# Attention probabilities brought to their keys' partitions by VectorE transposes and a copy through DRAM, in place of transposes by DMA

## The chip, the cores and the metric

The kernel runs on one core of a Trainium2 chip. A core has TensorE (PE: matmuls, with weight loads, PEld, beside them), VectorE (DVE), ScalarE (ACT), GpSimd (POOL) and SyncE (SP), which here only issues DMAs; 16 DMA engines move the data. Each engine works through its own instructions in order and waits on semaphores. The metric is the time of one execution on the device, in microseconds (us).

## The reference

One transformer layer on x of 2048 x 512 (f32): multi-head latent attention, a residual and a layer norm, then one linear layer with bias, a residual and a layer norm.

```python
cq = rms_norm(x @ w_qa.T)                                   # 2048 x 384
q_nope, q_pe = split((cq @ w_qb.T).reshape(s, 16, 192))     # 128 + 64 a head, rotary on q_pe
ckv_l, k_pe = rms_norm(...), rope(...)                      # of x @ w_kva.T: 128 + 64
k_nope, v = split((ckv_l @ w_kvb.T).reshape(s, 16, 256))
scores = (q_full @ k_full.T) * 192 ** -0.5                  # 16 heads, causal
out = softmax(scores) @ v @ w_o.T
x = layernorm(x + out)
x = layernorm(x + x @ (weight * scale_weight[:, None]).T + bias)
```

## The kernel before, in words

The keys' and values' up-projections are folded into the queries and the output, so scores are taken against the shared latent (`Kn`, 128 rows) and the rotary part (`Kp`), and the values are the latent itself (`V`). Every f32 operand of a matmul is split into a high and a low part; a score is five matmuls (`score`, L409 to L427, the matmuls on L421). The causal mask is added on the diagonal 128 columns either by a bf16 matmul in the middle of the five (L423: block 0, and block 3's first head of a pair) or by a VectorE addition in the score bank (L427).

Queries come in four **blocks** b of 512, heads in eight **pairs** p, and a block in four **query tiles** qt of 128. A tile needs nk = (4b + qt + 1) x 128 keys: 128 to 512 in block 0 and 1664 to 2048 in block 3. One (b, p, qt) is called a **unit** here. `units` (L626) runs over p, then qt, then the two heads j.

For a head in blocks 1 to 3, `head_scores` (L432) makes the scores, takes the negated maximum (L459, VectorE), the bias (L466 or L468), the exponentials into `pr` with their sums (L474, ScalarE), and the reciprocal of the sum (`inv`, L484 to L487). `head_probs` (L490) scales `pr` into f16 high words (L495, ScalarE) and the f16 remainder (L498, VectorE); both stand in one tile `hl`, first all high words, then all low words. Then one `dma_start_transpose` a head on SP (L502) moves `hl`, queries on partitions, into `PT`, keys on partitions. `head_probs` is a generator that is advanced while the next head's scores are made, so these steps interleave with the next head's maximum. In block 0, `pair_scores` and `pair_probs` (L507, L529) do the same for both heads at once, with the transpose on L535.

`values` (L540) multiplies V with both heads' words: for each 128 keys three matmuls of 256 columns (L551), in two halves, then a copy to `ot` (L556) and a store (`put_off`). A unit's product is put off: `run_values(lag)` runs half of an older unit's product after each head's scores, with a lag of 3, 3 and 2 units in blocks 1, 2 and 3. TensorE's queue therefore holds, in block 3: scores of unit u's first head, first half of the product of unit u-2, scores of the second head, second half, and so on. `PT` is a part of `ring`, 12 x 2048 half-words a partition, which holds three units in block 3.

The order is written by hand for TensorE and SP from block 1 on, and for VectorE and ScalarE too from block 3's second tile on; elsewhere the scheduler of the language orders VectorE and ScalarE. SP's queue holds, in order, the transposes, the `ot` stores and the loads of projected weights (`wq`, `wpe`).

After the last block an output stage runs from L770: it accumulates 512 columns for each 128 tokens over 8 pairs (`accumulate`), adds the residual, normalises (`layer_norm`, L847), transposes, applies the linear layer (`ffn`, L867) and normalises again. `rsqrt` (L193) is an addition and a power on GpSimd. In `ffn`, GpSimd adds bias and residual beforehand (`xb`, L874).

Of the kernel before, what the change touches and what calls it, by code (L numbers as in the profile page):

```python
# [9 lines left out]
F16 = mybir.dt.float16  # L10
BF16 = mybir.dt.bfloat16
F32 = mybir.dt.float32
F32R = mybir.dt.float32r
AF = mybir.ActivationFunctionType
ALU = mybir.AluOpType
# [34 lines left out]
def mla_block(ctx: ExitStack, tc: tile.TileContext, a, out):  # L50
# [45 lines left out]
    ctx_kv = ctx.enter_context(ExitStack())  # L96
    kv = ctx_kv.enter_context(tc.tile_pool(name="kv", bufs=1))
# [12 lines left out]

    blk = ctx.enter_context(tc.tile_pool(name="blk", bufs=2, side="right"))
# [72 lines left out]
    def value_output(p, pool, tag):  # L184

        wvo = state["wvo"][p]
        for j in range(2):
# [3 lines left out]
            yield  # L191

# [216 lines left out]
    def score(ps, c0, w, b, p, j, qt, masked):  # L409
# [7 lines left out]
        by_product = b == 0 or b == 3 and j == 0  # L417
        ops = [(qh, Kn, 0), (qh, Kn, 1), (ql, Kn, 0), (qp, Kp, 0), (qp, Kp, 1)]
        n = 0
        for lhs, K, i in ops:  # L420
            nc.tensor.matmul(ps[:, :w], lhs, K[:, i, c0 : c0 + w], start=n == 0, stop=n == 4)  # L421
            if n == 1 and masked is not None and by_product:
                nc.tensor.matmul(ps[:, masked : masked + P], identb, maskb, start=False, stop=False)  # L423
            n += 1
        if masked is not None and not by_product:
            dg = ps[:, masked : masked + P]
            nc.vector.tensor_tensor(dg, dg, maskb, ALU.add)  # L427
# [4 lines left out]
    def head_scores(pools, b, p, j, qt, nk, prev):  # L432
# [38 lines left out]
        pr = pools[1].tile([P, nk], F32, tag="pr", name=f"pr{b}_{p}_{qt}_{j}", bufs=4 if b == 1 else 2)  # L471
# [17 lines left out]

    def head_probs(pools, b, p, j, qt, nk, PT, pr, inv):  # L490
        hl = pools[0].tile([P, 2, nk], F16, tag="hl", name=f"hl{b}_{p}_{qt}_{j}", bufs=(6, 4, 2)[b - 1])
# [5 lines left out]
        for c in cuts:  # L497
# [3 lines left out]
        n2 = 2 * nk  # L501
        nc.sync.dma_start_transpose(  # L502
            PT[:, j * n2 : (j + 1) * n2].rearrange("p (k q) -> p k q", q=P), hl.rearrange("p a c -> p (a c)")
        )
        put_in()

    def pair_scores(pool, b, p, qt, nk):  # L507
# [4 lines left out]
        for j in range(2):  # L512
            score(ps[:, j, :], 0, w, b, p, j, qt, nk - P)
# [15 lines left out]
    def pair_probs(pool, b, p, qt, nk, PT, pr, inv):  # L529
        hl = pool.tile([P, 2, 2, nk], F16, tag=f"hl{qt}", name=f"hl{b}_{p}_{qt}")  # L530
        for j in range(2):
# [3 lines left out]
        nc.sync.dma_start_transpose(  # L535
            PT[:, : 4 * nk].rearrange("p (k q) -> p k q", q=P), hl.rearrange("p j a c -> p (j a c)")
        )
        yield

    def values(b, p, qt, nk, PT):  # L540

        kts = nk // P
        v = PT[:, : 4 * nk].rearrange("p (j a k q) -> p j a k q", j=2, a=2, k=kts)
# [297 lines left out]
    def load_fw(kt):  # L841
        raw = pc.tile([P, HID], F32, tag="xb", name=f"fraw{kt}", bufs=2)
        nc.scalar.dma_start(raw, a["fw"][:, kt])
        nc.vector.tensor_tensor(raw, raw, fsc, ALU.mult)
# [142 lines left out]
```

## Time and profile before

| | us |
|---|---|
| median of 3 runs | 1588.22 (1586.73 to 1588.98) |
| the profiled execution | 1588.17 |
| its span, first to last instruction | 1586.4 |

| part of the span | from | to | length |
|---|---|---|---|
| block 0, with the first projections | 0 | 253.6 | 253.6 |
| block 1 | 253.6 | 495.5 | 241.9 |
| block 2 | 495.5 | 851.9 | 356.4 |
| block 3 | 851.9 | 1328.7 | 476.8 |
| output stage | 1328.7 | 1586.4 | 257.7 |

A row of the groups reads: line, engine, operation, written tile <- read tiles, shapes (partitions x elements a partition), count | busy us in all, mean ns of one | idle time of the engine just before them, and what ended it. Matmuls overlap, so a mean duration (273 ns for a product with V) is longer than the distance from one start to the next (109 ns, taken from the starts in the trace). "SPq" rows are DMA issues; the transposes held SP's queue 3353 ns each in the median for `ring`. Of the 633,032 DMA packets 557,056 have 256 B: the transposes'. The granted TensorE clock was 0.993 in the mean.

### The profile page before, as it was taken

The numbers are of one execution on the slowest core, as the hardware profiler recorded it, in microseconds if no ns is written. First come the engines' busy times: TensorE is split into PE (matmuls) and PEld (weight loads), VectorE is DVE, ScalarE is ACT, GpSimd is POOL, SyncE is SP. The second block draws the span as 40 slices with busy tenths as digits, with TensorE's granted clock in tenths as the row PEclk, the third lists the DMA queues.
The fourth block names the chain that finished last, engine by engine and source line by source line (L and its number), as shares of the span: only waits on it lengthen the run. The fifth ranks groups of instructions, "written<-read, shape, count | busy, mean of one in ns | idle before, by whom it ended". The sixth has DMA issues, their size and how long they took to land. (4 is left out here: it accounts for less than half of the span.)

```text
span 1586.4 us, 24671 instructions
## 1 busy us (share of the span) xinstructions
PE 1546.3 (97%) x9130; PEld 1291.1 (81%) x9130; DVE 1161.2 (73%) x2099; ACT 924.7 (58%) x1631; POOL 361.5 (23%) x434
## 2 busy tenths in 40 slices
PE   8899998999999999999999999999999999999997
PEld 7688877888887788888888788888888886788886
DVE  6777777878787978787786877877777775465564
ACT  5767776665665676666765665665666665311120
POOL 2243325154016204050032401400400000022132
PEclk9999999999999999999999999999999999999999
DMA  7879877788897987788897888878678798433230
GB/s 230 258 197 240 191 191 160 147 176 190 149 218 163 173 163 165 159 162 170 160 204 148 168 145 168 156 143 165 140 143 176 148 233 196 146 118 122 94 113 33
DMA packets 633032, 262.49 MB, mean 165 GB/s; under 512 B 570288, under 2 KB 611376, under 8 KB 631888
## 3 DMA queue, kind: packets, MB, share of 16 engines
q1 hardware_dynamic: 621472, 233.62, 68.8%
q0 software_dynamic: 4672, 17.73, 3.6%
q10 hardware_dynamic: 6768, 9.57, 2.1%
q8 instruction: 72, 1.18, 0.3%
q14 instruction: 48, 0.39, 0.1%
HBM read 83.17 MB, written 35.13 MB: 75 GB/s over the span
## 5 line engine op out<-in xcount | busy, mean ns | idle before, releaser
L421 PE MATMUL s<-Kn,qn 128*128 128x512 f32 (+4 forms) x1920 | 521.1, 376 | 9.4 <-ACT pr L474 4.4
L474 ACT ACTIVATE pr<-s,bias,rq 128x1024 f32<-128x1024 f32 (+3 forms) x320 | 324.4, 1017 | 217.0 <-DVE bias L468 157.2
L498 DVE SCALAR_TENSOR_TENSOR hl<-pr,inv,hl 128x1024 f16<-128x1024 f32 (+7 forms) x320 | 359.6, 1137 | 38.7 <-ACT hl L495 34.9
L421 PEld LDWEIGHTS s<-Kn,qn 128*128 128x128 f32 x1920 | 339.5, 190 | 55.7 <-ACT pr L474 7.4
L551 PEld LDWEIGHTS <-V 128*128 128x128 f16 x3264 | 302.5, 98 | 86.6 <-issue 47.6
L551 PE MATMUL o<-ring,V 128*128 128x256 f16 x3024 | 362.9, 273 | 2.5 <-DVE qn L68 1.2
L421 PE MATMUL s<-Kp,pe 128*128 128x512 f32 (+4 forms) x1280 | 361.4, 363 | 0.0
L495 ACT ACTIVATE hl<-pr,inv 128x1024 f16<-128x1024 f32 (+7 forms) x320 | 294.6, 961 | 91.3 <-issue 34.5
L459 DVE TENSOR_REDUCE neg<-s 128x1 f32<-128x1024 f32 (+3 forms) x320 | 317.8, 993 | 38.0 <-PE s L421 34.9
L421 PEld LDWEIGHTS s<-Kp,pe 128*128 128x128 f32 x1280 | 234.0, 189 | 29.6
L359 POOL TENSOR_TENSOR prod<-prod 128x512 f32<-128x512 f32 x15 | 19.4, 1292 | 639.1 <-DVE prod L352 639.0
L391 PE MATMUL ps_qn<-cq,wq 128*128 128x512 f32 x576 | 145.1, 397 | 3.1 <-ACT ot L556 1.7
L770 PE MATMUL acc<-wvo,oh 128*128 128x512 f32 x448 | 143.9, 402 | 1.8 <-ACT pr L474 1.8
L374 POOL TENSOR_TENSOR pe<-prod,ph 32x512 fp32r<-32x512 f32 x92 | 138.8, 1509 | 6.0
L391 PEld LDWEIGHTS ps_qn<-cq,wq 128*128 128x128 f32 x576 | 107.3, 190 | 24.8 <-ACT ot L556 2.4
L770 PEld LDWEIGHTS acc<-wvo,oh 128*128 128x128 f32 x448 | 83.1, 188 | 23.2 <-issue 3.8
L486 DVE TENSOR_SCALAR inv<-sums 128x1 f32<-128x1 f32 x128 | 27.0, 211 | 97.5 <-ACT pr L474 97.5
L770 PE MATMUL acc<-wvo,ol 128*128 128x512 f32 x224 | 88.1, 393 | 0.0
L556 ACT ACTIVATE ot<-o 128x256 f32<-128x256 f32 x128 | 48.4, 378 | 45.2 <-PE o L551 39.6
L347 PE MATMUL ps_pe<-cq,wpe 128*128 128x512 f32 x288 | 73.8, 402 | 0.2 <-DMA cq<-cq_d 0.2
L64 ACT ACTIVATE oh<-o 128x1024 fp32r<-128x1024 f32 x28 | 29.7, 1060 | 65.6 <-PE acc L770 50.0
L65 DVE TENSOR_TENSOR ol<-o,oh 128x1024 fp32r<-128x1024 f32 x28 | 38.8, 1387 | 39.3 <-ACT oh L64 39.3
(147 smaller groups left out, 1631.6 us busy)
## 6 DMA issues: line engine op xcount, KB each, us to landing
wq<-wq_d SPq DMA_DIRECT2D x22, 768.0 KB, 5.7
o<-ot_d SPq DMA_DIRECT2D x32, 512.0 KB, 3.3
ot_d<-ot SPq DMA_DIRECT2D x97, 128.0 KB, 2.4
wpe<-wpe_d SPq DMA_DIRECT2D x10, 768.0 KB, 5.4
wq<-wq_d POOLq DMA_DIRECT2D x9, 768.0 KB, 6.4
cq_d<-cqst SPq DMA_DIRECT2D x18, 256.0 KB, 4.8
wo<-in_wo_dram SPq DMA_DIRECT2D x4, 1024.0 KB, 5.3
x<-in_x_dram SPq DMA_DIRECT2D x16, 256.0 KB, 3.7
```

The source lines that it names most:

```text
L65: nc.vector.tensor_tensor(l, ps, h.bitcast(F32), ALU.subtract)
L347: nc.tensor.matmul(ps, w[:, i, lt, x * P : (x + 1) * P], cq[:, k, lt, :], start=n == 0, stop=n == 8)
L374: (nc.gpsimd if not quick or (b, g) == (0, 0) and j % 2 else nc.vector).tensor_tensor(pe[64 + 32 * x : 96 + 32 * x, j, :], rp[q, x, :], ph ...
L391: nc.tensor.matmul(ps, w[:, i, lt, j * P : (j + 1) * P], cq[:, k, lt, :], start=n == 0, stop=n == 8)
L421: nc.tensor.matmul(ps[:, :w], lhs, K[:, i, c0 : c0 + w], start=n == 0, stop=n == 4)
L459: nc.vector.tensor_reduce(neg[:, ti : ti + 1], v, axis=AX.XY, op=ALU.max, negate=True)
L474: nc.scalar.activation(pr[:, c0 : c0 + n * w].rearrange("p (a c) -> p a c", a=n), v, AF.Exp, bias=bias, scale=r, accum_out=sums[:, ti : ti ...
L495: nc.scalar.activation(hl[:, 0, c], pr[:, c], AF.Copy, scale=inv)
L498: nc.vector.scalar_tensor_tensor(hl[:, 1, c], pr[:, c], inv, hl[:, 0, c], ALU.mult, ALU.subtract)
L551: nc.tensor.matmul(ps[:, :256], vt[:, i, k % 4, :], v[:, :, l, k, :], start=n == 0, stop=n == 3 * kts - 1)
L556: nc.scalar.activation(ot, ps[:, :256], AF.Copy)
L770: nc.tensor.matmul(acc, l[:, t, c], state["wvo"][p][:, i, j, :], start=p == 0 and j == 0 and n == 0, stop=p == NPAIR - 1 and j == 1 and n ...
```

## The change

The two halves of a probability, f16 high and f16 low, now lie side by side in one 32-bit word, so that a move of words moves both. VectorE transposes such words within squares of 32 x 32 (`turn`, into the `pr` tile, which is free by then), a DMA writes the squares to a DRAM tile `sq`, and, when both heads of a pair are written, four DMAs read it back, each filling 32 partitions of `PT` (`gather`). In `values` the moving operand then takes every second half-word.

```diff
+    def turn(words, sq, dst):
+        nc.vector.transpose(
+            sq.rearrange("p (k c r) -> p c k r", k=4, r=32), words.rearrange("p (c k r) -> p c k r", k=4, r=32)
+        )
+        nc.sync.dma_start(dst, sq.rearrange("p (k x) -> p k x", k=4))
+
+    def gather(PT, src):
+        for k in range(4):
+            nc.sync.dma_start(
+                PT[32 * k : 32 * k + 32].bitcast(F32).rearrange("p (q x) -> p q x", q=4),
+                src[:, k].rearrange("(q p) x -> p q x", q=4),
+            )
+
     def head_probs(pools, b, p, j, qt, nk, PT, pr, inv):
-        hl = pools[0].tile([P, 2, nk], F16, tag="hl", name=f"hl{b}_{p}_{qt}_{j}", bufs=(6, 4, 2)[b - 1])
+        words = pools[0].tile([P, nk], F32, tag="hl", name=f"hl{b}_{p}_{qt}_{j}", bufs=(4, 3, 2)[b - 1])
+        hl = words.bitcast(F16).rearrange("p (n a) -> p a n", a=2)
...
-        n2 = 2 * nk
-        nc.sync.dma_start_transpose(
-            PT[:, j * n2 : (j + 1) * n2].rearrange("p (k q) -> p k q", q=P), hl.rearrange("p a c -> p (a c)")
-        )
+        if j == 0:
+            state["sq"] = dram.tile([P, 4, nk // 2], F32, tag=f"sq{b}", name=f"sq{b}_{p}_{qt}", bufs=4)
+        sq = state["sq"]
+        turn(words, pr, sq[:, :, j * nk // 4 : (j + 1) * nk // 4])
+        if j == 1:
+            gather(PT, sq)
         put_in()
...
     def values(b, p, qt, nk, PT):
-        v = PT[:, : 4 * nk].rearrange("p (j a k q) -> p j a k q", j=2, a=2, k=kts)
+        v = PT[:, : 4 * nk].rearrange("p (q j k r a) -> p j a k q r", j=2, q=4, a=2, k=kts)
```

`pair_probs` changes likewise, with one transpose and one write for both heads. The number of `pr` tiles goes from 4, 2, 2 to 5, 3, 2 in blocks 1, 2 and 3, that of `hl` from 6, 4, 2 to 4, 3, 2. Two tiles of 32 B a partition (`pad_l`, `pad_r`) move all later tiles to multiples of 64 B.

The mask by matmul moves behind the five matmuls of a score; in block 0 both heads' scores come first, then both masks.

```diff
-            nc.tensor.matmul(ps[:, :w], lhs, K[:, i, c0 : c0 + w], start=n == 0, stop=n == 4)
-            if n == 1 and masked is not None and by_product:
-                nc.tensor.matmul(ps[:, masked : masked + P], identb, maskb, start=False, stop=False)
+            nc.tensor.matmul(ps[:, :w], lhs, K[:, i, c0 : c0 + w], start=n == 0, stop=n == 4 and not by_product)
+
+        def mask():
+            nc.tensor.matmul(ps[:, masked : masked + P], identb, maskb, start=False, stop=True)
```

In the output stage the value products are made for two pairs at a time (`value_outputs`, from pair 2 on), the residual of the linear layer is put into its weights (the identity is added to their diagonal squares), the bias is added with the matmul's result, and the addition in `rsqrt` of a layer norm goes to VectorE. The last tile gets its bias by two matmuls with one row, is normalised in two halves, and stored by SP and ScalarE.

```diff
+        dg = raw[:, kt * P : (kt + 1) * P]
+        nc.vector.tensor_tensor(dg, dg, ident, ALU.add)
...
-        rsqrt(r, mv[:, 1:2], 1, 1e-5)
-        nc.vector.tensor_scalar(dst, src, mv[:, 0:1], r, ALU.subtract, ALU.mult)
+        t = small.tile([P, 1], F32, tag="lnt", name="lnt")
+        nc.vector.tensor_scalar(t, mv[:, 1:2], 1e-5, None, ALU.add)
+        nc.gpsimd.tensor_tensor(r, t, nhalf[:, :1], ALU.pow)
+        for i in range(parts):
+            c = slice(i * HID // parts, (i + 1) * HID // parts)
+            nc.vector.tensor_scalar(dst[:, c], src[:, c], mv[:, 0:1], r, ALU.subtract, ALU.mult)
...
-        nc.gpsimd.tensor_tensor(xb, x1, fb, ALU.add)
...
-        nc.vector.tensor_tensor(xb, ps, xb, ALU.add)
-        layer_norm(xb, xb)
-        nc.sync.dma_start(out[0, t * P : (t + 1) * P, :], xb)
+        if not last:
+            nc.vector.tensor_tensor(xb, ps, fb, ALU.add)
+        layer_norm(xb, ps if last else xb, 2 if last else 1)
+        if last:
+            for i, q in enumerate((nc.sync, nc.scalar)):
+                c = slice(i * HID // 2, (i + 1) * HID // 2)
+                q.dma_start(out[0, t * P : (t + 1) * P, c], xb[:, c])
+        else:
+            nc.sync.dma_start(out[0, t * P : (t + 1) * P, :], xb)
```

## The prediction, made before the changed kernel had run

> **What bounds the kernel now.** I read the page's busy shares first, then the engines' busy time in windows cut at the query blocks, then the groups by line and shape, then the timeline around one product with V, and last how long DMAs take to land.
>
> ```profile
> PE 1546.3 (97%) x9130; PEld 1291.1 (81%) x9130; DVE 1161.2 (73%) x2099; ACT 924.7 (58%) x1631; POOL 361.5 (23%) x434
> ```
>
> ```profile
> 0.00:253.60 253.60, 233.68 (x1526) 200.58 (x1527) 186.01 (x435) 175.68 (x449) 81.72 (x154) 0.97 0.81 215
> 253.60:495.50 241.90, 239.09 (x1440) 202.80 (x1439) 194.78 (x415) 153.61 (x242) 81.65 (x72) 0.99 0.85 175
> 495.50:851.90 356.40, 353.76 (x2151) 298.05 (x2150) 291.64 (x543) 240.53 (x434) 83.16 (x72) 1.00 0.84 167
> 851.90:1328.70 476.80, 471.81 (x2883) 391.24 (x2881) 357.60 (x512) 299.29 (x438) 65.29 (x56) 1.00 0.80 159
> 1328.70:1550.00 221.30, 220.48 (x1013) 176.82 (x1014) 116.22 (x170) 53.82 (x66) 40.22 (x63) 1.00 0.41 131
> ```
>
> The windows are blocks 0 to 3 and the output stage; the columns are window, length, then busy time of PE, PEld, DVE, ACT, POOL, the granted clock, the DMA share and GB/s. TensorE fills 99% of blocks 1 to 3 (1065 of 1075 us) at full clock, and VectorE already 82% of block 2. So the transposes by DMA cost no time today: only work put in TensorE's way can move the end.
>
> ```profile
> L551 PE MATMUL o<-ring,V 128*128 128x256 f16 x3024 | 362.9, 273 | 2.5 <-DVE qn L68 1.2 <-DVE wvo L68 0.8 <-DMA ring<-hl 0.5
> L459 DVE TENSOR_REDUCE neg<-s 128x1 f32<-128x1024 f32 x144 | 175.4, 1218 | 35.8 <-PE s L421 34.9
> L498 DVE SCALAR_TENSOR_TENSOR hl<-pr,inv,hl 128x1024 f16<-128x1024 f32 x48 | 61.3, 1278 | 3.6 <-ACT hl L495 2.0
> ```
>
> The products wait 0.5 us in all for the transposed probabilities. How close that is, the timeline shows for block 3, pair 2, query tile 3 (nk = 2048):
>
> ```profile
> 1038.14 1.28 DVE L498 SCALAR_TENSOR_TENSOR hl<-pr,inv,hl 128x1024 f16<-128x1024 f32 x1
> ...
> 1039.45 5.54 SPq L502 DMA_TRANSPOSE ring<-hl  x1
> ...
> 1048.57 2.79 PE L551 MATMUL o<-ring,V 128*128 128x256 f16 x24
> ```
>
> The last half of the low words ends at 1039.42, the transpose is issued 0.03 us later, and the product starts at 1048.57: 9.15 us of slack, of which the DMA (landing 3.4 / 5.5 / 11.5 us, minimum, median, maximum, for `ring`) takes most. I followed the instructions in order and took this slack for all 96 units (block, pair, query tile) of blocks 1 to 3. Medians for query tiles 0 to 3: block 1: 12.9, 13.2, 6.9, 9.7 (five of tile 2 have 4.2 to 4.9); block 2: 20.3, 19.1, 16.6, 18.6; block 3: 14.0, 12.8, 10.2, 9.2. The program order of TensorE in blocks 1 to 3 is the same in both kernels except for 32 mask products, so the slack is all the new path gets.
>
> **The path of the words.** It was one DMA; it becomes a VectorE transpose, a write to DRAM, SP's wait for its landing, and four reads, each of which needs both heads. Landings that bear on it:
>
> ```profile
> o<-ot_d SPq DMA_DIRECT2D x32, 512.0 KB, 3.3
> ot_d<-ot SPq DMA_DIRECT2D x97, 128.0 KB, 2.4
> wo<-in_wo_dram SPq DMA_DIRECT2D x4, 1024.0 KB, 5.3
> ```
>
> 512 KB more cost 2.0 us more: 3.9 us a MB (262 GB/s) on 1.3 us fixed. A head's write is nk/2 KB, a pair's reads nk KB. With the transpose at nk/960 + 0.1 us (the reduce row: 1.22 us for 1024 elements, 1.14 from start to start) and 0.5 us for the issues, the path takes 3.2 + 6.9 us per 1000 of nk: 7.6, 8.5, 9.4, 10.3 us in block 1; 11.2 to 13.8 in block 2; 14.7, 15.6, 16.5, 17.3 in block 3. Against the slack, block 3's pair 2 lacks 1.1, 3.9, 6.2 and 8.2 us. TensorE then stands before the product, with all later scores queued behind it. A stall also gives the next unit as much more slack, as the next low words hang on scores already issued. So the stall is lack minus the stall before it: 0, 3.9, 2.3, 5.9. Summed over all units: 20 us in block 1, 0.5 in block 2, 76 in block 3.
>
> Here a rule speaks against the change. Each read fills 32 partitions. The Trainium skill ("SBUF — State Buffer", section "Door 1: The DMA port swizzle") says that 32 partitions reach 8 of 16 ports, measured at 189 GB/s for 1 MiB against 328 for 128 partitions. No DMA of this size here fills 32 partitions. By the rows block 3 loses 76 us; with reads at about 200 and writes at 330 GB/s 101 us (an estimate from that page), and block 1 25. If four queued reads pack the queue at the page's 435 GB/s, it is 18 and 10. I take 60 for block 3, a little under the rows, as they have one DMA at a time and four share the fixed part, and 18 for block 1.
>
> **VectorE.** The transposes carry nk elements a head: 16 x 3328, 16 x 5376, 16 x 7424 in blocks 1 to 3, or 55.5, 89.6, 123.7 us at 0.96 elements per ns, plus 64 x 0.07 to 0.13 us: 60 to 64, 94 to 98, 128 to 132. Counting the present instructions from start to start (about 0.083 us under their durations when packed), VectorE's present need is 179, 268 and 323 us; with the transposes 239 to 243, 362 to 366 and 452 to 455, against TensorE's windows of 241.9, 356.4 and 476.8. Block 2, which has slack for the path, becomes VectorE-bound: +6 to +10 at perfect packing, and I take +10. Block 1 is at its limit: +4 on top of the 18. Block 3 has room. Queued behind each transpose are the next head's `inv`, reciprocal and maximum; ScalarE's scaling waits for the first, the release of score banks for the last. In block 3 that falls into the 1.3 us in which VectorE waits for the exponentials. Block 0: 21 us of transposes in 253 at 73% load, and reads of 256 to 1024 B: +3, between -3 (its DMA share is 0.81) and +10.
>
> A second new wait: `pr` now holds the turned words until the write has landed, and block 3 has two of them. In the timeline around 1090 us the exponentials of a head of nk = 2048 start at 1089.29, its low words end at 1097.00, and the exponentials of the head after next, which take its `pr`, start at 1103.77. With 2.2 for the transpose and 5.3 for the write `pr` comes free near 1104.7: 0.9 us late, while score banks stay full and the scaling of the same head queues behind on ScalarE. It concerns heads of nk = 1920 and 2048 (32 of 64), and a stall before a product makes room for it: between 0 and +25, I take +5. Blocks 1 and 2 have 5 and 3 buffers: 0.
>
> **TensorE reading every second half-word.** A product's moving operand now steps 4 bytes. The nearest row is the 256-column score matmul of 4-byte elements, which takes 119 ns from start to start against the product's 109: 3264 x 10 ns = +33 us. The Trainium skill (same page, "Specifications (TRN2)") puts full bandwidth at two or more hits per 16-byte line, and a 4-byte step makes four: 0. The extra 10 ns stand with a 190 ns weight load (98 ns for f16), so I take 0 and keep 33 as the upper end. No reason gives a gain.
>
> **SP, DMA, ScalarE.** SP loses transpose issues of 3.35 us median and gets one write and two reads a head at about 0.55: less time, though it now waits for each second write to land; behind it stand the `ot` stores and weight loads, needed units later: 0. DMA bytes: 142.6 MB of transposed words become as much written and as much read, in packets of 640 to 4096 B instead of 557,056 of 256 B; the share (0.80 to 0.85) should stay below 0.9: 0, and if the port rule holds, up to +30 in block 2. ScalarE writes half-words at a 4-byte step, same count: 0. Pads: 0.
>
> **Mask, output stage.** A bf16 mask in the middle of a score makes the next f32 matmul start 0.08 us later; moved to the end or shared by two heads it saves about 0.08 x 64: -5. The output stage is TensorE-bound (220.5 of 221.3), so leaving GpSimd's `xb` addition out (1.38 us x16, covered by the next tiles), and giving VectorE 32 additions of an epsilon and four of the identity (half of it idle there), is worth nothing until the last tile, whose chain loses one addition (0.69) and splits its store, and gains two small bias products: -1. Paired value products: same count, 0.
>
> **Sum.** The profiled execution took 1588.17 us (span 1586.4 and 1.8 around it), level with the median of 1588.22. 60 + 18 + 4 + 10 + 5 + 3 - 5 - 1 = +94: 1682 us.
>
> **Rivals.**
> - The port rule holds in full: 101 + 25 + 4 + 10 to 40 + 5 + 3 - 6 = +142 to +172, near 1745. For it: the rule is measured. Against it: four reads of both port halves are in the queue together.
> - The path is nearly hidden: reads pack at 435 GB/s. Stalls 18 + 10, VectorE 14, the rest -3: +39, or 1627, down to 1600 if VectorE's packing costs nothing and block 1's order gives more slack. For it: packets of 4 KB. Against it: even then nk = 2048 needs 12.6 us where 9.2 are.
> - Faster: freed of 557,056 small packets, DMAs in block 0 (share 0.81) land earlier. TensorE's 20 us of idle time there shrinks by 12, the mask gives 5 and the last tile 1: about 1570. This decides only if the path fits into 9.2 us at nk = 2048, that is if write and reads together take under 7 us for 3 MB (over 430 GB/s with nothing fixed). I see no room for that.
> - The change doesn't take effect: excluded, VectorE's order holds the 224 transposes.
>
> **Chances.** Forecast 0.47, port rule 0.22, nearly hidden 0.24, faster 0.05, no difference 0.02. The range of 1600 to 1750 takes in most of the second and third cases. A measurement of this kernel tells 0.2% (3 us) from no change: faster 0.05, same 0.02, slower 0.93.
>
> **What would show it.** Right: idle time of PE before the product with V, released by the DMA into `ring`, largest in block 3 and growing from query tile 0 to 3; little in block 2, where VectorE is over 95% busy; product matmuls still 109 ns apart; reads landing 7 to 9 us after issue. Wrong: reads landing under 5 us, block 3 under 495 us, products over 115 ns apart, transposes over 1.3 us for 1024 words, or idle time behind SP's wait that delays weights.

## The result and the profile after

The changed kernel took 1969.74 us (median of 4 runs, 1966.13 to 1974.57), the kernel before 1588.60 beside it: a ratio of 1.240, 95% interval 1.2368 to 1.2432. That is 381 us more where the forecast had 94. The profiled execution has a span of 1972.8 us.

The page's busy shares and the windows by block (columns as before; block 3 is cut here at the first product of the output stage, 3 us earlier than in the prediction):

```profile
PE 1658.8 (84%) x9132; PEld 1348.4 (68%) x9132; DVE 1476.3 (75%) x2360; ACT 999.6 (51%) x1633; POOL 330.6 (17%) x386
```

```profile
0.00:285.60 285.60, 242.38 (x1532) 208.51 (x1533) 209.12 (x466) 181.55 (x449) 82.23 (x154) 0.95 0.70 226
285.60:607.80 322.20, 259.23 (x1428) 214.78 (x1427) 252.86 (x478) 166.60 (x241) 80.07 (x72) 0.91 0.75 211
607.80:1071.80 464.00, 394.94 (x2180) 320.60 (x2180) 385.80 (x611) 264.44 (x437) 82.63 (x72) 0.93 0.81 223
1071.80:1697.50 625.70, 509.92 (x2856) 404.31 (x2854) 488.87 (x568) 328.62 (x433) 64.86 (x56) 0.91 0.78 214
1697.50:1972.80 275.30, 252.30 (x1146) 200.24 (x1143) 139.70 (x242) 58.39 (x74) 20.84 (x32) 0.97 0.40 127
```

The loss is 32, 80, 108, 152 and 14 us by stage. TensorE falls from 99% to 80 to 85% of blocks 1 to 3, and no other engine takes its place: VectorE has 78, 83 and 78%. Nothing is full. Of the 340 us more in blocks 1 to 3, 239 are time in which TensorE stands (9 before, 248 now), and 101 are longer TensorE work: the clock that it was granted was 0.99 and more before and is 0.91 to 0.93 now. The forecast had no term for that. The groups by line and shape:

```profile
L589 PE MATMUL o<-ring,V 128*128 128x256 f16 x3024 | 412.1, 292 | 172.1 <-DMA ring<-sq 145.4 <-DVE wvo L68 12.6 <-ACT ot L594 3.9
...
L477 DVE TENSOR_REDUCE neg<-s 128x1 f32<-128x1024 f32 x144 | 174.8, 1214 | 40.7 <-PE s L433 39.9
...
L533 DVE SCALAR_TENSOR_TENSOR hl<-pr,inv,hl 128x1024 f16<-128x1024 f32 x48 | 69.0, 1439 | 14.7 <-ACT hl L530 14.7
...
L511 DVE STREAM_TRANSPOSE pr<-hl 128x1024 f32<-128x1024 f32 x24 | 29.7, 1239 | 0.0
```

The product's wait for `ring` went from 0.5 to 145 us. A transpose costs what was forecast (1239 ns for 1024 words); the low words became dearer (1278 to 1439 ns). The same unit as in the prediction, block 3, pair 2, query tile 3, in the timeline (VectorE's, SP's, ScalarE's and TensorE's lines around the turn):

```profile
1310.84 1.42 DVE L533 SCALAR_TENSOR_TENSOR hl<-pr,inv,hl 128x1024 f16<-128x1024 f32 x1
...
1312.21 1.21 ACT L492 ACTIVATE pr<-s,bias,rq 128x1024 f32<-128x1024 f32 x1 [2.43 <-DMA sq<-pr]
...
1312.29 2.31 DVE L511 STREAM_TRANSPOSE pr<-hl 128x2048 f32<-128x2048 f32 x1
...
1314.63 0.53 SPq L514 DMA_DIRECT2D sq<-pr  x1
...
1319.18 1.74 SPq L519 DMA_DIRECT2D ring<-sq  x4
...
1331.56 3.62 PE L589 MATMUL o<-ring,V 128*128 128x256 f16 x19 [7.28 <-DMA ring<-sq]
```

From the low words' end (1312.26) to the product are 19.3 us; it was 9.15, and the forecast's formula has 17.3. The turn takes 2.3, the write lands 4.4 after its issue, the last of the four reads 12.2 after the first one's issue, and the product starts 0.1 later, with 7.28 us of TensorE idle in front. The two windows behind that gap show what it does to the clock (the third number from the end):

```profile
1327.60:1334.40 6.80, 2.84 (x14) 1.99 (x15) 2.00 (x2) 0.75 (x1) 0.00 (x0) 0.50 1.02 304
1334.50:1341.30 6.80, 6.80 (x39) 5.90 (x38) 3.53 (x6) 3.88 (x6) 0.00 (x0) 1.00 0.74 170
```

In the first, products start 213 ns apart, behind it 111 ns. In blocks 1 to 3 the trace has 239 us at a clock of 0.50 (3 before), in which TensorE was busy for 173 us. Half of that, about 86 us, is an estimate of what the clock costs there; the 4 ns more between products at full clock (below) are another 13 us or so.

The landings (destination, source, count, KB each, median us from issue to landing):

```profile
sq<-pr SPq DMA_DIRECT2D x16, 1024.0 KB, 5.0
ring<-sq SPq DMA_DIRECT2D x32, 512.0 KB, 8.4
o<-ot_d SPq DMA_DIRECT2D x32, 512.0 KB, 3.7
```

I followed all 96 units this way. Means in us, before / after; "forecast" is the prediction's formula:

| stretch of a unit | block 1 | block 2 | block 3 |
|---|---|---|---|
| last score ends to low words end | 8.5 / 11.9 | 9.4 / 16.9 | 11.1 / 12.4 |
| low words end to words landed | 5.2 / 13.7 | 5.7 / 16.5 | 6.7 / 18.7 |
| the same, forecast | 8.9 | 12.5 | 16.0 |
| landed to product starts | 6.2 / 1.6 | 13.3 / 2.3 | 5.4 / 1.3 |
| sum: last score to product | 19.9 / 27.2 | 28.4 / 35.8 | 23.2 / 32.4 |
| from product to product | 7.9 / 10.6 | 11.0 / 14.5 | 14.9 / 20.1 |

Products now follow their landing almost at once. What else waits, in block 2 and in block 3 (who for whom, us in all, times, longest):

```profile
PEld s L433 <- ACT pr L492: 72.8, 30, 8.3
PE s L433 <- ACT pr L492: 64.1, 27, 8.0
ACT ot L594 <- DMA ot_d<-ot: 50.0, 20, 4.5
ACT pr L492 <- DVE bias L486: 44.2, 15, 7.0
ACT pr L492 <- DMA sq<-pr: 43.7, 17, 6.4
```

```profile
ACT pr L492 <- DMA sq<-pr: 146.2, 29, 12.0
...
PE o L589 <- DMA ring<-sq: 97.8, 20, 9.0
```

In block 2 it is the scores that wait, for the exponentials to free the score banks (`s`, in PSUM, where TensorE's results lie); in block 3 it is the products. Four theories came out of this. **V**: VectorE's added work. **B**: the reads fill 32 partitions and are slow for it, at half rate by the rule in the prediction. **H**: `pr` is held until its write has landed, and SP's queue stands behind the wait for it (called Q where the queue alone is meant). **P**: the path from the last score to the product, divided by the units that TensorE's order puts between them (2.5, 2.5 and 1.6, the sum over the pitch in the table).

### The profile page after: what moved, and what is told of

It reads as the page before. It is cut to its first block, busy times and chain, and to the rows that moved or that the text cites. A ratio compares the mean times of both kernels' runs of the same rounds, so it can differ in the third digit from the quotient of the medians.

```text
span 1972.8 us, 25801 instructions
## 1 busy us (share of the span) xinstructions
PE 1658.8 (84%) x9132; PEld 1348.4 (68%) x9132; DVE 1476.3 (75%) x2360; ACT 999.6 (51%) x1633; POOL 330.6 (17%) x386
## 4 chain that ended last, share of the span: by engine, by line
PE 24%; DMA 19%; DVE 17%; ACT 5%; issue 2%; SPq 1%; POOL 0%; ACTq 0%; POOLq 0%; DVEq 0%
DMA sq<-pr 14%; PE acc L808 8%; PE s L433 7%; DVE hl L533 6%; DVE pr L511 5%; PE o L589 5%; DMA ring<-sq 4%; DVE neg L477 4%; ACT pr L492 2%; PE ff L929 2%; ACT hl L530 2%; PE ps_qn L403 1%; SPq L519 1%; PE ps_pe L359 0%; DMA o<-ot_d 0%
## 5 line engine op out<-in xcount | busy, mean ns | idle before, releaser
L433 PE MATMUL s<-Kn,qn 128*128 128x512 f32 (+4 forms) x1920 | 540.9, 391 | 91.5 <-ACT pr L492 80.5
L589 PE MATMUL o<-ring,V 128*128 128x256 f16 x3024 | 412.1, 292 | 172.1 <-DMA ring<-sq 145.4
L433 PEld LDWEIGHTS s<-Kn,qn 128*128 128x128 f32 x1920 | 357.2, 201 | 154.2 <-ACT pr L492 95.7
L533 DVE SCALAR_TENSOR_TENSOR hl<-pr,inv,hl 128x1024 f16<-128x1024 f32 (+7 forms) x320 | 391.0, 1235 | 51.9 <-ACT hl L530 51.5
L530 ACT ACTIVATE hl<-pr,inv 128x1024 f16<-128x1024 f32 (+7 forms) x320 | 363.3, 1196 | 115.5 <-DVE inv L505 113.7
L433 PE MATMUL s<-Kp,pe 128*128 128x512 f32 (+4 forms) x1280 | 378.1, 377 | 0.0
L477 DVE TENSOR_REDUCE neg<-s 128x1 f32<-128x1024 f32 (+4 forms) x320 | 315.9, 988 | 45.2 <-PE s L433 43.1
L511 DVE STREAM_TRANSPOSE pr<-hl 128x256 f32<-128x256 f32 (+6 forms) x224 | 328.8, 1469 | 2.6
L433 PEld LDWEIGHTS s<-Kp,pe 128*128 128x128 f32 x1280 | 248.1, 200 | 32.5
L371 POOL TENSOR_TENSOR prod<-prod 128x512 f32<-128x512 f32 x15 | 19.3, 1284 | 904.1 <-DVE prod L364 904.0
L445 DVE TENSOR_TENSOR s<-s,maskb 128x128 f32<-128x128 f32 x160 | 47.2, 295 | 36.1 <-PE s L433 35.8
```

What stands on the lines that cost most here:

```text
L477: nc.vector.tensor_reduce(neg[:, ti : ti + 1], v, axis=AX.XY, op=ALU.max, negate=True)
L511: nc.vector.transpose(sq.rearrange("p (k c r) -> p c k r", k=4, r=32), words.rearrange("p (c k r) -> p c k r", k=4, r=32))
L530: nc.scalar.activation(hl[:, 0, c], pr[:, c], AF.Copy, scale=inv)
L533: nc.vector.scalar_tensor_tensor(hl[:, 1, c], pr[:, c], inv, hl[:, 0, c], ALU.mult, ALU.subtract)
L589: nc.tensor.matmul(ps[:, :256], vt[:, i, k % 4, :], v[:, :, l, k, :], start=n == 0, stop=n == 3 * kts - 1)
```

## The experiments

Time is the median of two runs (four for the first two rows, more for rest_only and out_only) beside the kernel before on the same chip; the stages are from one profiled execution each, cut at VectorE's first maximum of a block and at the first product of the output stage. An execution can differ from its kernel's median: the changed kernel's stages add up to 3 us more than its median, those of gather_128 and gather_old to 7 and 5 us less.

| kernel | time | block 0 | 1 | 2 | 3 | output |
|---|---|---|---|---|---|---|
| before | 1588.6 | 253.6 | 241.9 | 356.4 | 473.4 | 261.0 |
| changed | 1969.7 | 285.6 | 322.2 | 464.0 | 625.7 | 275.3 |
| rest_only | 1591.4 | 257.9 | 240.7 | 356.4 | 472.2 | 261.1 |
| out_only | 1587.8 | 253.3 | 242.2 | 356.5 | 473.3 | 260.5 |
| dve_load | 1708.8 | 257.8 | 258.5 | 424.9 | 496.5 | 267.3 |
| before_in_order | 1638.2 | 253.5 | 251.1 | 396.4 | 473.6 | 261.3 |
| turns_in_order | 1730.6 | 260.9 | 292.3 | 411.8 | 498.1 | 266.3 |
| no_turn | 1859.5 | 267.8 | 311.6 | 422.5 | 592.7 | 261.1 |
| gather_128 | 1906.5 | 280.6 | 318.2 | 447.5 | 579.4 | 273.8 |
| gather_old | 1920.4 | 284.1 | 301.4 | 445.5 | 609.2 | 275.0 |
| in_place | 1932.2 | 283.4 | 323.5 | 440.3 | 622.1 | 265.0 |
| contiguous | 1958.1 | 279.3 | 321.0 | 458.8 | 620.4 | 275.4 |
| all_four | 1786.8 | 281.4 | 281.7 | 408.2 | 545.4 | 272.6 |
| all_in_place | 1760.4 | 277.1 | 282.5 | 404.8 | 528.2 | 264.8 |
| pr_free | 2002.7 | 281.7 | 345.2 | 469.3 | 634.1 | 269.6 |
| pool_queue | 2045.7 | 301.1 | 350.8 | 466.6 | 645.5 | 280.0 |
| gather_head | 2057.9 | 276.3 | 372.1 | 513.7 | 612.4 | 279.0 |
| ot_scalar | 1967.2 | 283.4 | 311.4 | 469.0 | 627.5 | 276.2 |
| more_lag | 1987.3 | 289.6 | 322.0 | 461.7 | 645.8 | 276.2 |
| more_lag_pr | 1973.0 | 281.6 | 324.0 | 450.7 | 641.2 | 274.7 |

The last two leave block 3's code as it is and yet have it 16 to 20 us longer; so a difference of that size in one block of one kernel is not read as a cause, and the split by blocks below is a hint where it is smaller. more_lag's two runs lie 20 us apart, so its total says nothing either way.

### VectorE's turns alone, and everything but them

dve_load adds to the kernel before (its `turn` is the VectorE transpose alone, without a DMA; block 0 has the same line for a pair):

```diff
+        turn(hl.rearrange("p a c -> p (a c)").bitcast(F32), pr)
         n2 = 2 * nk
         nc.sync.dma_start_transpose(
```

> The kernel before plus the VectorE transposes alone: each head's words are also turned into its pr tile, nothing reads the result, the product still takes the DMA transpose's words. Theory V (VectorE's load is the lost time): 1750 or more, since VectorE gets about 315 us more work in blocks 0 to 3. Theory H (the write that is waited for) and B (the reading back at half rate): only the sums of the prediction, +17 plus the ends of blocks, so 1600 to 1625.

+119 us, between the theories. Block 2 takes 68 of it. Its window, and one of its waits:

```profile
516.30:941.20 424.90, 379.63 (x2179) 313.22 (x2178) 379.98 (x611) 240.27 (x436) 81.79 (x72) 0.95 0.70 141
```

```profile
ACT pr L474 <- DVE pr L491: 40.2, 13, 4.3
```

VectorE and TensorE are each busy for 380 of 425 us: neither is full. The kernel before has two `pr` tiles in this block, and here the exponentials wait 40 us for a turn to leave one; the changed kernel has three, so dve_load is not quite the turn of the changed kernel. no_turn is the other half, the changed kernel without the transpose:

```diff
-        nc.vector.transpose(
-            sq.rearrange("p (k c r) -> p c k r", k=4, r=32), words.rearrange("p (c k r) -> p c k r", k=4, r=32)
-        )
-        nc.sync.dma_start(dst, sq.rearrange("p (k x) -> p k x", k=4))
+        nc.sync.dma_start(dst, words.rearrange("p (k x) -> p k x", k=4))
```

> The changed kernel without VectorE's 32x32 turns: the words are written to DRAM as they are (output not the reference's), all transfers stay, pr is free early. Theory P: block 3 loses the turn's 2.15 us of path and about 0.5 of VectorE's queue, over 1.6, 32 times, so 50; block 1 some 3 us over 2.5, so 40; block 2, where scores wait for the exponentials in their two PSUM buffers and the reductions stand behind the turns, 65 to 100: 1780 to 1815. If VectorE is not what holds block 2: that block stays above 430 us and the whole above 1850.

1859.5, above the expectation: what is left, the transfers above all, costs 271 us. No stage moved as far as was said: block 2 by 42 (65 to 100 expected), block 3 by 33 (50), block 1 by 11 (40). no_turn writes from `hl`, so it also leaves `pr` free early, and its 110 us are two things. The kernel in_place (below) tells them apart: it leaves `pr` free too and has the turns. So from the kernel before to the changed one there are three steps: 271 for the transfers with all the rest of the change (no_turn), 73 for the turns beside them (in_place less no_turn), 38 for holding `pr` (changed less in_place). In another order the steps could have other sizes; the larger part is the transfers either way.

### Does block 2 lack VectorE time, or its order?

Both kernels put VectorE and ScalarE in the order as written from block 1 on; turns_in_order also has dve_load's edit, before_in_order is the kernel before with the order alone:

```diff
-    with tc.manual_schedule(engines={ET.PE, ET.SP}), ExitStack() as ctx_f:
+    with tc.manual_schedule(engines={ET.PE, ET.SP, ET.DVE, ET.Activation}), ExitStack() as ctx_f:
```

> The kernel before plus VectorE's turns (nothing reads them), with VectorE and ScalarE in the order as written in blocks 1 and 2 too, so that a head's turn stands behind the next head's bias in place of ahead of its reductions. VectorE's work is unchanged. Theory O (where the turns stand in the queue): block 2 falls from 425 to 380 to 400, 1665 to 1690 in all. Theory V (the sum of VectorE's work): block 2 stays at 415 or more, 1700 or more.

> Control for the one above: the kernel before with VectorE and ScalarE in the order as written in blocks 1 and 2. TensorE has 99% there and the path has slack, so nothing: 1585 to 1595.

The control failed its expectation (1638, not 1585 to 1595), and that tells more than the test, which fell between its two marks in block 2 (412) and on V's side in all (1731). Block 2 of before_in_order and of turns_in_order:

```profile
504.60:901.00 396.40, 367.40 (x2160) 302.53 (x2159) 293.52 (x546) 244.42 (x436) 82.12 (x72) 0.98 0.75 151
```

```profile
553.20:965.00 411.80, 367.46 (x2165) 302.94 (x2164) 385.77 (x609) 245.32 (x436) 82.13 (x72) 0.98 0.72 146
```

An order alone costs block 2 40 us with VectorE at 74%. Adding 92 us of turns in this order costs 15 more, where in the other order they cost 68. In block 1 it is the other way round: 41 us in this order (251.1 to 292.3), 17 in the other. So the same turns cost 15 to 68 us in a block according to what stands around them in the queue; the sum of VectorE's work doesn't give the price. The traces show where it goes in block 2: from a head's last score to its exponentials are 3.1 us in the mean in the kernel before and 6.8 in dve_load, 4.8 and 5.4 in the two kernels in order. What stands in VectorE's queue ahead of the maximum holds the exponentials, and with them the score banks.

The sum is not out of it, though. With the turns VectorE is busy for 380 us of the block, and 386 of 412 in turns_in_order; a block of 356 us couldn't hold that. A full VectorE would explain 24 of the 68 us; the other 44 are waits. How much of those is order and how much comes of the two `pr` tiles, no run here separates.

### The reads: partitions, and the wait for the write

```diff
+        n = src.shape[2]
+        to = PT.bitcast(F32)
         for k in range(4):
-            nc.sync.dma_start(
-                PT[32 * k : 32 * k + 32].bitcast(F32).rearrange("p (q x) -> p q x", q=4),
-                src[:, k].rearrange("(q p) x -> p q x", q=4),
-            )
+            nc.sync.dma_start(to[:, k * n : (k + 1) * n], src[:, k])
```

> The changed kernel with the same bytes, packets and number of reads, but each read fills all 128 partitions with a quarter of their columns in place of 32 partitions with all of them (so the words go to other places than the product needs: the output is not the reference's). Theory B: a 512 KB read lands in about 5 us in place of 8.4 and the time falls by 150 us or more, to 1820 or less. Theory H: reads land faster, but pr still waits for its write and the queue for its landing; 1880 to 1940.

```profile
ring<-sq SPq DMA_DIRECT2D x32, 512.0 KB, 6.2
```

The same bytes in the same packets land in 6.2 in place of 8.4 us; 63 us less. Most of it (46 of 73 between the two profiled executions) is in block 3, where the four reads of a unit take 8.0 in place of 11.25 us in the mean. B's mechanism holds, its size (150) does not; 1906 lies in H's range.

```diff
-            gather(PT, sq)
+            gather(PT, state.get(("old", nk), sq))
+            state["old", nk] = sq
```

> The changed kernel with eight DRAM buffers a block, and each read taking the words that the same query tile of the head pair before had written (the first pair reads its own), so that the read waits for no write that is just under way: output not the reference's, same bytes, packets, reads and turns. Theory H: SyncE's 493 us of waiting for the write goes, reads start 4 to 5 us earlier and the product's wait for the ring (145 us) nearly vanishes; pr still waits for its write; 1780 to 1850. Theory B: transfers stay as slow as they are; 1920 or more.

-49 us, in the profiled executions about 20 in each of blocks 1 to 3: just on B's mark, 70 above H's range. SP is freed (in block 1 it waits 20 us for landings in place of 137), but the reads of a block 3 unit, now issued beside the writes, take 13.7 us in place of 11.25 from the first issue to the last landing.

### The held `pr`

pr_free, then in_place:

```diff
-        nc.sync.dma_start(dst, sq.rearrange("p (k x) -> p k x", k=4))
+        src = sq.rearrange("p (k x) -> p k x", k=4)
+        nc.sync.dma_start(dst[:, :, :8], src[:, :, :8])
+        src = Kn.rearrange("p a c -> p (a c)").bitcast(F32)[:, : sq.shape[1]].rearrange("p (k x) -> p k x", k=4)
+        nc.sync.dma_start(dst[:, :, 8:], src[:, :, 8:])
```

```diff
-        turn(words, pr, sq[:, :, j * nk // 4 : (j + 1) * nk // 4])
+        turn(words, words, sq[:, :, j * nk // 4 : (j + 1) * nk // 4])
```

> The changed kernel, but in blocks 1 to 3 a write takes only the first 8 of its nk/4 words a row from the turned tile (a small transfer ahead) and the bulk from the key tile, which is never overwritten there: same bytes to DRAM, one more issue a head, output not the reference's. The pr tile is then free after the small write. Theory H (held tile): ScalarE's 193 us of waiting for the write goes; block 3 loses 60 us or more of its 626, block 2 some 25; 1860 to 1900 in all. If the time is set by VectorE's and ScalarE's own chain or by late reads, the wait only changes its name: 1940 or more.

> The changed kernel, but in blocks 1 to 3 VectorE turns each head's words in their own tile and the write reads that tile, so pr is free after the low words, as it was before (the places inside the tile then no longer match: output not the reference's; all durations, bytes and waits for landing stay). Theory H (pr held until its write lands; ScalarE waited 193 us for it): 1900 or less. Theory P (in block 3 the pace is the path from a unit's last score to its product divided by the 1.6 units that lie between, and the held tile's own loop, 16.8 us of every 20.1, has room): 1950 to 1970, the wait vanishing from ScalarE without a gain.

pr_free went up to 2002.7 and is no test of its question: its small writes, in rows of 32 B, landed no sooner, and ScalarE still waited 144 us for them. in_place gains 38 us, more than P and less than H foresaw: 24 in block 2, 10 at the start of the output stage, 4 in block 3. In block 3 the 146 us of waiting only changed its name:

```profile
ACT pr L492 <- DVE bias L486: 178.0, 61, 7.6
```

So ScalarE's longest wait cost next to nothing, and one a third as long (44 us in block 2), in the way of scores, some 24. more_lag_pr gives block 2 a fourth `pr`: ScalarE's wait for the write goes from 44 to 1 us there, and the block gains 11 to 13, half of it. A gain of that size in one block is not clear of the differences named above.

### The half-words' 4-byte step

```diff
-        hl = words.bitcast(F16).rearrange("p (n a) -> p a n", a=2)
+        hl = words.bitcast(F16).rearrange("p (a n) -> p a n", a=2)
...
-        v = PT[:, : 4 * nk].rearrange("p (q j k r a) -> p j a k q r", j=2, q=4, a=2, k=kts)
+        v = PT[:, : 4 * nk].rearrange("p (a q j k r) -> p j a k q r", j=2, q=4, a=2, k=kts)
```

> The changed kernel with the two half-words kept apart (high halves, then low halves) in place of interleaved, and the product reading 32 contiguous values at a time: the turned words then mean nothing, output not the reference's; bytes, turns and transfers unchanged. Frees the 4-byte step: ScalarE's copies back to 961 ns (-70 us busy), VectorE's low words to 1278 ns at 1024 (-31 us), products from 113 to 109 ns. Theory V (the chain through ScalarE and VectorE sets the pace): 60 us or more less, 1910 or less. Theory H: 20 to 30 less, 1940 to 1950. The prediction's zero: 1960 to 1970.

```profile
L533 DVE SCALAR_TENSOR_TENSOR hl<-pr,inv,hl 128x1024 f16<-128x1024 f32 x48 | 62.4, 1303 | 10.6 <-ACT hl L530 10.6
...
L530 ACT ACTIVATE hl<-pr,inv 128x1024 f16<-128x1024 f32 x48 | 53.3, 1141 | 15.9 <-DVE inv L505 15.7
```

ScalarE's copy falls back from 1445 to 1141 ns, the low words from 1439 to 1303, the products from 113 to 109 ns apart. Together they are worth 12 us, close to the "prediction's zero" and far from V's 60: ScalarE and VectorE have room.

### Four together

The edits of gather_128, gather_old and contiguous in one kernel, with that of pr_free (all_four) or that of in_place (all_in_place).

> The changed kernel with four things taken away together: reads fill 128 partitions, reads take the words of the pair before, pr is held by the small write only, half-words lie apart. Output not the reference's; the bytes and VectorE's turns stay. If the loss is the turns on VectorE (119 us by themselves) plus these four, it falls to 1700 to 1740. Over 1780 there is a cause that none of my kernels has yet touched.

> Reads over all 128 partitions, from the pair before, half-words apart, turns in place (output not the reference's; bytes and VectorE's work stay). Theory P: block 3's path loses the write's landing (5.2), some 3 of the reads, 0.6 at ScalarE: 32.4 falls to about 24, over 1.55, 15.6 us a unit, 500 in the block; block 2 about the 425 and block 1 about the 260 of the kernel with the turns alone; 1715 to 1755 in all. Over 1780 something else remains.

all_four stays at 1786.8, just over its mark, and carries pr_free's extra writes. all_in_place takes away 209 us, where one by one these give 63 + 49 + 12 + 38 = 162. It ends 5 us above what P foresaw and 52 above the turns alone: 19 more in block 0 (where only the wide reads and the parted half-words apply), 24 in block 1, 32 in block 3, but 20 less in block 2 and 3 less in the output stage.

### SP's queue

pool_queue, gather_head (whose `gather_head` is `gather` over one head's columns) and ot_scalar:

```diff
-            nc.sync.dma_start(
+            nc.gpsimd.dma_start(
                 PT[32 * k : 32 * k + 32].bitcast(F32).rearrange("p (q x) -> p q x", q=4),
```

```diff
-        if j == 1:
-            gather(PT, sq)
+        gather_head(PT, sq, j)
```

```diff
         if state["queue"] is nc.gpsimd:
             nc.gpsimd.dma_start(dst, src)
+        elif n == 0 and src.shape[1] == 256 and len(src.shape) == 2:
+            nc.scalar.dma_start(dst, src)
```

> The changed kernel (output as it should be) with the four reads of a unit issued by GpSimd's queue in place of SyncE's, so that no write, store or weight load stands behind a read that waits for its write. Theory Q (SyncE's queue is the loss): ScalarE's 108 us of waiting for stores of o goes and writes start at the end of their turn; 1880 to 1920. If the queue only passes on what is late anyway: 1950 to 1970. GpSimd building the reads' descriptors could cost more than SyncE's waiting did: 1990 or more.

> The changed kernel (output as it should be) with the reading back cut by heads: four reads of half the bytes after each head's write, so that only the second head's half is left when the unit's last write lands. Theory P: block 3's reads take about 7 in place of 11.25 us of the path, over 1.6, so 80 less; block 1 about 25 less; block 2, paced by PSUM, 0 to 10 less: 1845 to 1885. If the four more issues and their waits block SyncE's queue for more than that: 1970 or more.

> The changed kernel (output as it should be) with the stores of o in blocks 1 to 3 issued from ScalarE's queue, right behind the copy that makes them, in place of SyncE's. Theory Q (SyncE's queue, where reads wait for their write and their ring slot, holds the stores back, and so ScalarE's next copy): ScalarE's 108 us of waiting for these stores go, the exponentials and high halves of blocks 1 and 2 come earlier; 20 to 45 less, 1925 to 1950. If the copies were waiting in slack: 1960 to 1975.

gather_head was meant to shorten the path and lost 88 us, 50 each in blocks 1 and 2. SP's own waits in block 1, the changed kernel's first, then gather_head's:

```profile
SPq L519 <- DMA sq<-pr: 137.0, 33, 9.4
SPq L514 <- DVE pr L511: 51.3, 21, 6.4
```

```profile
SPq L528 <- DMA sq<-pr: 192.9, 60, 10.2
SPq L514 <- DVE pr L511: 6.3, 2, 5.8
```

In the changed kernel SP spends 137 of block 1's 322 us waiting for writes to land and waits for the engines only 64 us; most of the rest is issuing (112). With twice the reads, each unit has twice the waits and twice the reads' issues (149 us of issuing in block 1): SP is hardly ever idle (10 of 372 us), and the second head's write starts 12.6 us after its turn. Which of the two, waits or issues, costs the 50 us was not separated. GpSimd is no way out (76 us more in all): its queue, too, stands while a read waits for its write (138 us in block 1), behind and ahead of the rotary work. The stores of `ot` cost nothing that shows: ot_scalar is 2.5 us under the changed kernel, inside the spread of its runs.

### Is block 1 paced by the path?

The ring has room for six units in block 1; more_lag_pr also raises block 2's `pr` tiles from 3 to 4.

```diff
-        lag = min(ring.shape[1] // (2048 * (b + 1)) - 1, 3) if b else 2
+        lag = min(ring.shape[1] // (2048 * (b + 1)) - 1, 5) if b else 2
```

> The changed kernel (output as it should be) with products in block 1 two units later in TensorE's order: 4.5 in place of 2.5 units after their scores, all six places of the ring in use; blocks 2 and 3 unchanged. Theory P (path over distance): 27.2 us of path over 4.5 is 6.0, under the 7.9 of TensorE's own work, so the path sets nothing any more and block 1 falls from 322 to what VectorE's turns alone left, 258, or somewhat over it: 260 to 285, 1910 to 1935 in all. If VectorE, ScalarE or the queues pace block 1: 305 or more, 1955 to 1975.

> As more_lag, with a fourth pr tile in block 2 in place of three (output as it should be). If the held tile is what the turns in place won there: block 2 falls from 464 to about 440 and ScalarE's 44 us of waiting for the write in it to under 10; 1885 to 1910 in all. If it was something else, block 2 stays at 460 or more.

P falls for block 1. There the words now land 16 us before their product, and the block takes 322.0 us, as in the changed kernel. SP waits for the engines 48 us there, 15% of the block, and ScalarE 78 us for stores of `ot`. SP's queue fits this, and gather_old, which frees it, gains 21 in block 1; but no kernel here frees the queue and moves the products at once, so what paces block 1 is not shown.

### The other parts of the change

rest_only is the changed kernel with the turn undone, out_only is the kernel before with the last part of the diff, from `load_fw` on, and the paired value products.

> The kernel before with every other part of the change (mask order of block 0, the 32-byte pads, the output stage) and without the turn: the DMA transpose, contiguous half-words and old buffer counts stay. My sum: 6 us less than before, 1582, block 3 unchanged within 1 us. If these parts cost (rival: the pads or the mask order disturb block 0), 1590 or more. Either way they can't hold the 381 us.

> The kernel before with the output stage's edits alone (no pads, no mask order, no turn; output as it should be). The forecast gave them 1 to 5 us: 1583 to 1588. With all other parts together the time was 1591.4 and block 0 took 257.9 in place of 253.6: if mask order or pads cost that, block 0 is back at 253.6 here.

rest_only: ratio 1.0012 (1.0004 to 1.0021), block 0 4.3 us longer. out_only: 0.9991 (0.9985 to 0.9998), 1.4 us less, block 0 at 253.3. So mask order or pads seem to cost block 0 some 4 us (which of the two was not tried), and the output stage's edits gain about 1, less than 0.2%.

## Why the prediction was wrong, step by step

- **What bounds the kernel.** Right: TensorE at 99%, and all that came was time in which it stands or runs slower. The sign follows from that. The signs named for "right" came too (a wait before the products, longest in block 3; reads landing in 8.4 us), but they did not tell 94 us from 381.
- **The path, 60 in block 3, 18 in block 1: mis-sized, the largest miss in us.** The forecast had 78 us for the transfers, with SP's waits at 0; no_turn puts them, with the half-words' step, at 269 (271 less 2 for the rest). The mechanism is there in block 3: the product's wait for `ring`, 98 us in that block. Four terms of the sum were short. The landings (1.3 us + 3.9 a MB) came from rows of a stage with a DMA share of 0.4; at 0.75 to 0.81 the reads took 11.25 where the formula has 8.5 (block 3), and block 1's second writes 4.9 where it has 2.9. The slack was taken as usable to zero; 1.3 us of it stayed. The low words were taken as ready when they were before; they came 1.3 us later in block 3, 3.4 in block 1, 7.5 in block 2. And "the stall is lack minus the stall before it" hands each stall back to the next unit; with every unit late, 9.1 us of path became 5.2 us a unit. Block 1's 80 us go down by nothing when the path is given 16 us of room (more_lag), so there it isn't what paces, or not alone.
- **The port rule, weighed and set aside.** gather_128 agrees with it in direction: 8.4 against 6.2 us, 63 us in all. My argument against it, that four queued reads use both halves of the ports, is the one that the same page of the Trainium skill ("SBUF — State Buffer", section "Can I just issue two DMAs to hit both halves?") rejects. The 63 are what the rival had over the forecast (1745 less 1682), and by blocks as well: 41, 7 and 0 to 30 us more in blocks 3, 1 and 2 were foreseen, 46, 4 and 17 came back. It still ends 225 us short.
- **VectorE, +10 and +4: the step whose reasoning failed, not only its size.** "VectorE-bound: +6 to +10 at perfect packing" took the engine as a sum of work. Beside the transfers the turns cost 73 us, and alone in the old kernel 119, 68 of them in block 2, with VectorE at 89%; in the changed kernel it has 83%, where I wrote "over 95%". I had named the queue (the next head's `inv` and maximum behind each transpose, the score banks behind those) and priced it at nothing. The sum was low too: 362 to 366 us for block 2, where dve_load's VectorE was busy for 380.
- **The clock, no term.** The forecast had TensorE "at full clock" and let it stand without a price. The standing brought some 86 us (estimate above) of work at half the clock, about a quarter of the loss in blocks 1 to 3. The sizes of the other terms, taken from whole kernels, contain their share of it.
- **`pr`, +5: right wait, wrong place.** It cost 38, hardly any of it in block 3. Block 2, which I gave 0 for its three buffers, pays up to 24, and the output stage 10: there TensorE waits 12.6 us for `wvo`, and ScalarE, which makes it, 11.8 us for a last write of words.
- **SP, 0: wrong.** "Less time, though it now waits for each second write": the waits are its time. In block 1 it waits 137 of 322 us for landings and has only 64 in which it waits for an engine. Reading the words of an older write, which leaves these waits out, gains 49 us (gather_old). That the queue takes the place of the path in block 1 fits the runs and is not shown.
- **Half-words, 0: wrong by 12.** Products stand 113 ns apart (the upper end had 119), and ScalarE's copies cost 27% more, which I gave no range. Whether 16-byte lines explain the products no run shows; the rule of two hits a line, on which I took 0, did not hold to the last 4 ns.
- **Block 0, +3: wrong by 29.** The turns alone bring 4, the changed kernel without turns 14 (rest_only has 4 of these), both together 32. I didn't take it apart.
- **Mask, output stage, pads, -6: wrong by 8.** +2, of which -1.4 is the output stage.

By size: transfers and the rest 271, turns 73, the held `pr` 38. Of the transfers the narrow reads took 63, waiting for the write 49 and the half-words' step 12 when each was taken away alone; all three together with the 38 for `pr` give back 209, not 162. Open stay block 0, how path and queue share block 1, what order and what tiles cost in block 2, and 52 us between all_in_place and the turns alone.

## What to carry to other kernels

Before an engine is called free, ask what stands behind the new instruction in its queue and which buffer that releases; a busy share alone does not tell: at 74%, a mere order of the same work cost 40 us in one block. A copy through DRAM puts a wait for landing on a queue: count the queue's waits as its work, and take landing times from a stage as loaded as the one that will pay them. Rank waits by who waits last: 146 us of idle ScalarE in block 3 cost about 4, 44 in block 2 up to 24. And where TensorE begins to stand, look at the clock that it is granted afterwards: here about a quarter of the loss in blocks 1 to 3 is put down to half the clock, by the estimate above.

## What the hardware showed that I had not expected

- f16 words written at a 4-byte step cost ScalarE 1445 ns where side by side they cost 1141 (128 x 1024), VectorE 1439 against 1303; a 256-column product whose moving operand has that step takes 113 ns against 109.
- Four queued reads of 416 to 512 KB into 32 partitions each land in 11.25 us from the first issue (mean of block 3), 128 partitions wide in 8.0.
- Issued from GpSimd, a read holds that engine for 551 ns (median), from SP's queue 424.
- TensorE's clock was granted in steps of 3.41 us, at 1.00 or 0.50. One wait of 1.97 us was enough to lose half of it: TensorE was busy for 1.45 us of the first of these two windows, and the second ran at 0.50.

```profile
760.99:764.40 3.41, 1.45 (x9) 0.99 (x8) 0.39 (x4) 2.14 (x5) 0.00 (x0) 1.00 0.61 216
764.40:767.80 3.40, 3.40 (x9) 2.62 (x8) 3.31 (x7) 3.40 (x4) 0.00 (x0) 0.50 0.56 140
```

In the changed kernel's trace each of the 49 falls to 0.50 follows a step in which TensorE was busy for 1.53 us or less, and none follows the 444 steps at full clock with 1.54 us or more. In seven other kernels of the record the border is less sharp: some falls follow up to 1.84 us, and some steps of 1.40 us have none.
